# The second attention's keys and values projected during self-attention, and one output product moved ahead of the raw transposes

## The chip, the cores and the metric

The kernel runs on one core of one Trainium2 chip. Times are device microseconds (us) of one execution of the whole kernel; the figure that counts is the median over several executions. Engine names are those of the profile: PE is the matrix engine (PEld its weight loads), DVE the vector engine, ACT the scalar (activation) engine, POOL the GpSimd engine, and SP the engine that issues most of the transfers.

## The reference: what is computed

Two transformer layers over `x` of 16 batches x 128 tokens x 256 features, with a context tensor `ctx_2048` of the same shape:

```
x = x + tanh(g_xattn[0]) * L0_xattn(layernorm(x), ctx_2048)   # 16 heads of 128, self and cross
x = x + tanh(g_ffn[0])   * L0_ffn(layernorm(x))               # gated FFN, 704 wide
x = x + tanh(g_xattn[1]) * L1_xattn(layernorm(x), ctx_2048)   # 32 heads of 8, causal
x = x + tanh(g_ffn[1])   * L1_ffn(layernorm(x))               # top-1 of 8 experts, capacity 256
```

`L0_xattn` attends twice: once to the tokens themselves and once to the context; both results are concatenated, rounded to fp8 and multiplied by `wproj`. `L1_xattn` is the *second attention* of the title. It has 8 key and value groups of 8 features each, 4 query heads to a group. Cut to what matters here:

```
q = (Q @ w_q.T).reshape(B, S, 8, 4, 8)       # Q is the normed x
k = (K @ w_k.T).reshape(B, S, 8, 8)          # K is ctx_2048
v = (V @ w_v.T).reshape(B, S, 8, 8)          # V is ctx_2048
scores = einsum('bnghd,bmgd->bnghm', q, k) / sqrt(8)      # padding and causal mask
out = einsum('bnghm,bmgd->bnghd', softmax(scores), v)
return out @ w_o.T + b_o
```

So the keys and values of the second attention depend on the context and two weights alone, and on nothing that the kernel computes before.

## The kernel before

**Self- and cross-attention (lines 239 to 665).** The work is cut into 32 units: units 0 to 15 are the self-attention of one batch each, units 16 to 31 the cross-attention. A unit takes four steps; the loop at line 626 counts steps `n` from -11 to 135, so that unit u has its scores in the steps n = 4u to 4u+3. Each step handles four heads (`c`, 0 to 3) as a software pipeline: `scores`, `top` (row maximum), `exp`, one step later `recip` and `divide`, two steps later `probs` (transposes of the weights), three later `values`, `smooth` and `quant`, four later `quant_last` (which writes `cat` on POOL), five later `output` (the product with `wproj`, summed over the 16 heads of a unit in one accumulator). Ahead of its scores, a unit is projected in eight blocks of 512 columns, two in a step (`project`, `evict`, `bn`: blocks 0 and 1 are keys, 2 to 5 queries, 6 and 7 values), from step 4u-5 on. When blocks 0 to 5 have their statistics, `rstd` (step 4u-2, a chain of small DVE operations that ends in `q_r`) gives the scale of every head, `mult` (line 454, POOL) applies it to the *raw* blocks, and `heads` (line 463) transposes the raw blocks on PE, keys in step 4u-1, queries in the steps after. These are the "raw transposes".

`output` is called at the end of each step, after `heads`, `heads_q` and the second projection block:

```
            if ab[1]:
                ab[1][0].project(ab[1][1])
                ...
            do(n, 5, "output")
            once(n, 8, "residual")
```

In a step with n % 4 == 3, `output` handles c = 2 of the unit that is one and a half units behind; its operand `cat` is written by the `quant_last` of that same step.

**Order.** The functions are called in the order written out by hand in this loop. The tile framework turns that into one in-order queue for each engine, with semaphores between them; as the trace shows, an engine's order is that of the calls except where the framework let an operation go ahead (in the steps n % 4 == 3, for instance, one projection product stands ahead of the score products although it is called after them). Accumulators live in PSUM pools: two buffers `mm` for projections, two `tr` for transposes, two `sc` for scores, one `pv`, one `acc`.

**First FFN (lines 674 to 732, and 1083 to 1092)**: four groups of four batches, `gate_up` and `down`. In its second group the second attention's first group of four batches is prepared by `front_step`.

**Second attention (lines 904 to 1141).** The loop at line 1107 runs over 64 steps, four to a batch, each with eight heads: `scores`, `top`, `probs` of the step before, `exp`, and in every second step `values`. Every 16 steps a group of four batches is prepared ahead of its use by `front_step`: `load` (context and mask), `norm`, `turn`, and four calls of `qk` (line 949), which project queries (`aq`) and keys (`ak`, in which each key row stands four times, once for each query head of its group). `keys(b)` spreads a batch's keys over the heads with `hmask` (POOL, line 975), projects its values with `av` (line 981), and copies them into one of two padded tiles `vpads` (DVE, line 986). `output` and the `route` generators follow.

**Second FFN (lines 1149 to 1195)**: eight experts, tokens gathered and scattered through HBM.

Of the kernel before, what the change touches and what calls it, by code (L numbers as in the profile page):

```python
# [18 lines left out]
P = 128  # L19
# [16 lines left out]
def flamingo_kernel(  # L36
# [194 lines left out]

    xqx = dram.tile([B, P, KD * P], F32, name="xqx")
    x1 = dram.tile([B, P, DM], F32, name="x1")
    NU = 2 * B


# [2 lines left out]
    with (  # L239
# [346 lines left out]
        units = [Unit(u) for u in range(NU)]  # L586


        loads = {}

        def at(n, f, *args):
# [34 lines left out]
        for n in range(first, last + 1):  # L626
            for m in range(0, B, 4):
                if n == 4 * m - 11:
                    stats(m // 4)
            once(n, -8, "load")  # L630
            for f, args in loads.get(n, ()):
                f(*args)
            ab = [front(n, i) for i in range(2)]
            do(n, 1, "recip")
            do(n, 4, "quant_last")
            do(n, 1, "divide")
            do(n, 0, "scores")
# [233 lines left out]

# [32 lines left out]
    front = {}  # L904

    def load(g):
        cT = gp.tile([P, KD, NT], F32, tag="cT", name="cT")
        nc.gpsimd.dma_start(out=cT, in_=kpn(ctxT)[:, :, g * NT : (g + 1) * NT])
        mi = gp.tile([P, NT], I32, tag="mi", name="mi", bufs=1)
        nc.sync.dma_start(  # L910
            out=mi, in_=mask[g * NT : (g + 1) * NT].partition_broadcast(P)
        )
        comb = gp.tile([P, G, P], BF16, tag="comb", name="comb")
        pad = gp.tile([P, NT], F32, tag="pad", name="pad", bufs=1)
        nc.vector.tensor_scalar(pad, mi, 0.0, NEG, ALU.is_equal, ALU.mult)
# [4 lines left out]
        front[g] = {"cT": cT, "comb": comb}  # L920

    def norm(g):
        rows = [x[b] for b in range(g * G, (g + 1) * G)]
# [22 lines left out]
            nc.scalar.copy(hT[:, k, :], pt.rearrange("p n t -> p (n t)"))  # L946
        front[g]["hT"] = hT

    def qk(g, i, c):

        f = front[g]
        if c == 0:
            f[i] = gp.tile([P, KD, NT], F32, tag="qk"[i], name="qk"[i] + "T")
# [7 lines left out]
        if i == 0:  # L961
            nc.scalar.activation(f[i][:, c, :], pm, AF.Copy, scale=SCALE1)
        else:
            nc.scalar.copy(f[i][:, c, :], pm)

    kbs, vps, es, eTs, oTs, scs, mxs = {}, {}, {}, {}, {}, {}, {}

    def keys(b):
# [4 lines left out]
        kb = ap.tile([P, KD, NQ, P], F32, tag="kb", name="kb")  # L973
        for c in range(KD):
            nc.gpsimd.tensor_tensor(  # L975
                kb[:, c], f[1][:, c, None, tok].to_broadcast([P, NQ, P]),
                hmask[:, :, None].to_broadcast([P, NQ, P]), ALU.mult,
            )
        pm = psum.tile([P, NG, HD], F32, tag="mm", name="ps_mm")
        for k in range(KD):  # L980
            nc.tensor.matmul(
                pm, f["cT"][:, k, tok], av[:, k, :], start=(k == 0), stop=(k == KD - 1)
            )
# [3 lines left out]
        kbs[b], vps[b] = kb, vp  # L987

    def scores(n):

# [10 lines left out]
        with tc.high_priority(offset=100):  # L1001
            for i in range(2):
                rows = slice(32 * (2 * p + i), 32 * (2 * p + i) + 32)
                nc.tensor.matmul(  # L1004
                    s[:, i], f[0][rows, c, tok], kbs[b][rows, c], start=False, stop=True
                )
        scs[n] = s

# [64 lines left out]
    def front_step(g, i):  # L1073
# [193 lines left out]
```

## Time and profile before

| | us |
|---|---|
| median of 3 runs | 1542.24 (1539.53 to 1543.59) |
| the profiled execution | 1540.11 |
| its span in the profile | 1538.2 |
| PE busy | 1388.1 |
| DVE busy | 1052.2 |
| ACT busy | 814.6 |
| POOL busy | 669.5 |

The first score product of self-attention starts at 63.7 us of the span, the first cross product with the context at 473.9, the last output product of cross-attention at 947.6; the first FFN begins at 955.6, the second attention's first scores at 1079.6, its last value products at about 1388; the first gather of the second FFN is issued at 1408.1.

How to read it: the span is what the profiler saw of one execution; the time is measured outside it, in that execution 1.9 us more. Busy time is the union of an engine's instructions, matmul ends are modelled, and the matrix engine's granted clock is given as a share of full speed. The profile's timeline merges neighbouring instructions of one kind (`x4` is four of them) and puts in brackets how long the engine sat idle before them and whose result ended that.

### The profile page before, as it was taken

What the parts mean: (1) busy time and instruction counts of PE and PEld (TensorE: products, weight loads), DVE (VectorE), ACT (ScalarE), POOL (GpSimd) and SP (SyncE); (2) the same over time, 40 slices, a digit from 0 to 9 for tenths busy, and PEclk for the clock granted to TensorE, in tenths of its full rate; (3) what the DMA queues carried; (4) which work ended last, traced back from release to release, by engine and by line L of the source; (5) the groups of instructions that cost most, each with busy time, mean ns of one, the idle gap of its engine ahead of it and who ended that gap; (6) DMA issues with size and microseconds to landing.
All of it is one profiled execution on the core that took longest, in us unless ns stands there. A gap on an engine that the chain in (4) does not pass through costs nothing. (4 is left out here: it accounts for less than half of the span.)

```text
span 1538.2 us, 24640 instructions
## 1 busy us (share of the span) xinstructions
PE 1388.1 (90%) x8612; PEld 1009.7 (66%) x8612; DVE 1052.2 (68%) x2788; ACT 814.6 (53%) x2421; POOL 669.5 (44%) x574
## 2 busy tenths in 40 slices
PE   2778889798897999999999986999999999996998
PEld 1567677677675677777777764555556666664887
DVE  8888878878789777676767765433579797883100
ACT  3656566566556676666666662353355454542121
POOL 4576666666766555556565554120021312111111
PEclk9799999999999999999999998999999999996999
DMA  4300000000013100000000003400210100001662
GB/s 122 112 7 18 28 11 32 15 11 22 11 45 100 44 23 22 11 19 15 18 15 18 8 8 110 141 1 0 83 49 9 50 9 36 9 36 63 194 198 67
DMA packets 51115, 68.67 MB, mean 45 GB/s; under 512 B 5291, under 2 KB 37739, under 8 KB 50992
## 3 DMA queue, kind: packets, MB, share of 16 engines
q1 hardware_dynamic: 36912, 41.31, 9.1%
q10 hardware_dynamic: 11456, 17.63, 3.6%
q0 software_dynamic: 2624, 8.16, 1.5%
q8 instruction: 68, 1.11, 0.3%
q14 instruction: 55, 0.45, 0.1%
HBM read 50.53 MB, written 16.81 MB: 44 GB/s over the span
## 5 line engine op out<-in xcount | busy, mean ns | idle before, releaser
L509 POOL TENSOR_TENSOR e<-e,sums 128x512 f32<-128x512 f32 x128 | 139.7, 1092 | 230.8 <-DVE sums L505 120.8
L497 ACT ACTIVATE e<-ps_sc,mx 128x128 f32<-128x128 f32 x512 | 181.3, 368 | 90.1 <-DVE mx L489 82.7
L454 POOL TENSOR_TENSOR raw<-raw,q_r 128x512 f32<-128x512 f32 x192 | 207.9, 1112 | 34.1 <-DVE q_r L180 33.0
L431 DVE BATCH_NORM_STATS2 q_st<-raw 128x6 f32<-128x128 f32 x768 | 174.1, 279 | 66.9 <-ACT raw L422 66.5
L1020 ACT ACTIVATE e<-ps_sc,mx 128x128 f32<-128x128 f32 x512 | 139.7, 384 | 119.1 <-DVE mx L1011 114.1
L565 PE MATMUL ps_acc<-wp,cat 128*128 128x512 f32 x512 | 160.4, 436 | 17.6 <-POOL cat L227 15.5
L463 PE MATMUL ps_tr<-ident,raw 128*128 128x128 f32 x768 | 121.9, 288 | 46.0 <-POOL raw L454 43.8
L227 POOL TENSOR_TENSOR cat<-e_t,e_e 128x1024 fp32r<-128x1024 bf16 x64 | 136.2, 2128 | 53.7 <-DVE e_t L221 52.1
L481 PE MATMUL ps_sc<-kT,qT 128*128 128x128 f32 x1024 | 140.3, 280 | 15.0 <-ACT qT L472 15.0
L481 PEld LDWEIGHTS ps_sc<-kT,qT 128*128 128x128 f32 x1024 | 131.1, 193 | 33.0 <-ACT qT L472 27.0
L463 PEld LDWEIGHTS ps_tr<-ident,raw 128*128 128x128 f32 x768 | 96.0, 147 | 83.3 <-POOL raw L454 58.2
L519 ACT COPY eT<-ps_tr 128x512 f32<-128x512 f32 x128 | 75.4, 589 | 139.0 <-PE ps_tr L517 138.9
L975 POOL TENSOR_TENSOR kb<-kT,hmask 128x512 f32<-128x512 f32 x32 | 33.6, 1067 | 243.9 <-PE ps_sc L1004 184.6
L565 PEld LDWEIGHTS ps_acc<-wp,cat 128*128 128x128 f32 x512 | 95.9, 194 | 57.4 <-POOL cat L227 22.2
L527 PE MATMUL ps_pv<-eT,vt 128*128 128x256 f32 x512 | 132.1, 379 | 1.0 <-DVE cat_y L538 1.0
L422 ACT COPY raw<-ps_mm 128x512 f32<-128x512 f32 x192 | 113.7, 593 | 27.9 <-PE ps_mm L410 24.8
L527 PEld LDWEIGHTS ps_pv<-eT,vt 128*128 128x128 f32 x512 | 95.9, 189 | 31.2 <-issue 9.0
L538 DVE TENSOR_TENSOR cat_y<-ps_pv,r_sm 128x512 bf16<-128x512 f32 x128 | 87.1, 680 | 39.7 <-PE ps_pv L527 39.5
L472 ACT ACTIVATE qT<-ps_tr,hv 128x512 f32<-128x512 f32 x128 | 100.9, 789 | 21.8 <-PE ps_tr L463 19.8
L497 ACT ACTIVATION_READ_ACCUMULATOR e<-ps_sc,mx 128x1 f32 x512 | 105.3, 206 | 0.0
L489 DVE TENSOR_REDUCE mx<-ps_sc 128x4 f32<-128x512 f32 x128 | 87.2, 681 | 23.6 <-PE ps_sc L481 23.6
L1011 DVE TENSOR_REDUCE mx<-ps_sc 128x8 f32<-128x1024 f32 x64 | 78.2, 1222 | 25.0 <-PE ps_sc L1004 23.4
(228 smaller groups left out, 2807.3 us busy)
## 6 DMA issues: line engine op xcount, KB each, us to landing
w1t<-in_w ACTq DMA_DIRECT2D x8, 1024.0 KB, 5.0
w2t<-in_w ACTq DMA_DIRECT2D x8, 1024.0 KB, 5.6
disp<-empty SPq DMA_DIRECT2D x16, 257.0 KB, 8.5
xe<-disp SPq DMA_DIRECT2D x8, 514.0 KB, 3.6
stage<-in_wprojT SPq DMA_DIRECT2D x16, 256.0 KB, 2.7
xg<-in_x SPq DMA_DIRECT2D x4, 512.0 KB, 3.9
xb<-in_x SPq DMA_DIRECT2D x16, 128.0 KB, 2.1
ctx<-in_ctxT SPq DMA_DIRECT2D x16, 128.0 KB, 2.2
```

The costliest lines, as they stand in the source:

```text
L227: nc.gpsimd.tensor_tensor(dst, t[:, part], e[:, part], ALU.subtract)
L422: nc.scalar.copy(raw.rearrange("p h d -> p (h d)"), pm)
L431: nc.vector.bn_stats(self.st[:, 4 * blk + j, :], self.raws[blk][:, j, :])
L454: nc.gpsimd.tensor_tensor(src, src, self.r[:, 4 * blk : 4 * blk + 4, None].to_broadcast([P, 4, P]), ALU.mult,)
L463: nc.tensor.transpose(pt[:, j, :], src[:, j, :], ident)
L472: nc.scalar.activation(dst, pt, AF.Identity, scale=hv[:, col : col + 1], bias=hv[:, col + 1 : col + 2])
L481: nc.tensor.matmul(pscore[:, j, :], qT[:, j, :], self.kT[:, 2 * c + j // 2, :], start=True, stop=True,)
L497: nc.scalar.activation(e[:, j, :], pscore[:, j, :], AF.Exp, bias=self.mx[:, j : j + 1], accum_out=sums[:, j : j + 1],)
L509: nc.gpsimd.tensor_tensor(e, e, sums[:, :, None].to_broadcast([P, 4, P]), ALU.mult)
L527: nc.tensor.matmul(pv[:, 2 * g : 2 * g + 2, :], self.vt[:, gg * P : (gg + 1) * P], eT[:, 2 * g : 2 * g + 2, :], start=True, stop=True,)
L565: nc.tensor.matmul(self.acc, self.cat[c // 2][:, h % 8, :], wpr[self.cross, c][:, j, :, :], start=(h == 0), stop=(h == 15),)
L1020: nc.scalar.activation(e[:, i, :], s[:, i // NQ, i % NQ, :], AF.Exp, bias=mx[:, i : i + 1])
```

## The change

It has two parts.

1. Keys and values of the second attention are projected inside the loop of self- and cross-attention, one batch at a time, by a new function `kv1(b)`, called in step 4b+3 for the batches 0 to 14 and in step 61 for batch 15, after the first projection block and the statistics, and before `rstd` and the raw transposes. Four steps earlier `load_kv1` loads that batch's context (before batch 0 also the weights; of `akT` only one of the four equal copies of each row). The results are copied out by ACT and stored to two new tensors in HBM, `k1s` and `v1s`. The second attention reads them back: for each group of four batches 16 transfers of eight partitions each repeat the keys for the four heads, and one transfer brings the values. `qk` becomes `queries` and projects queries alone; `keys` loses its products, and its four DVE copies become one POOL copy with a repeated source.
2. In the steps with n % 4 == 3, `output` is called after `rstd` and before `mult` and `heads`; in the other steps it stays where it was.

```diff
+    k1s = dram.tile([NG * HD, B * P], F32, name="k1s")
+    v1s = dram.tile([B * P, NG * HD], F32, name="v1s")
...
+        ak = ap.tile([P, KD, NG * HD], F32, tag="ak", name="ak", bufs=1)
+        av = ap.tile([P, KD, NG * HD], F32, tag="av", name="av", bufs=1)
+        cxs = {}
+        kv1_at = {4 * b + 3: b for b in range(B - 1)}
+        kv1_at[4 * (B - 1) + 1] = B - 1
+
+        def load_kv1(b):
+            if b == 0:
+                for k in range(KD):
+                    nc.sync.dma_start(
+                        out=ak[:, k].rearrange("p (g d) -> p g d", d=HD),
+                        in_=akT[k * P : (k + 1) * P, :].rearrange(
+                            "p (g h d) -> p g h d", h=NH // NG, d=HD
+                        )[:, :, 0, :],
+                    )
+                nc.sync.dma_start(out=av, in_=kpn(avT))
+            cxs[b] = ap.tile([P, KD, P], F32, tag="ctx", name="ctx")
+            nc.sync.dma_start(out=cxs[b], in_=kpn(ctxT)[:, :, b * P : (b + 1) * P])
+
+        def kv1(b):
+            cx = cxs.pop(b)
+            tok = slice(b * P, (b + 1) * P)
+            pm = ps_mm([P, P + NG * HD])
+            for k in range(KD):
+                nc.tensor.matmul(
+                    pm[: NG * HD, :P], ak[:, k, :], cx[:, k, :], start=(k == 0), stop=(k == KD - 1)
+                )
+            for k in range(KD):
+                nc.tensor.matmul(
+                    pm[:, P:], cx[:, k, :], av[:, k, :], start=(k == 0), stop=(k == KD - 1)
+                )
+            ko = ap.tile([NG * HD, P], F32, tag="ko", name="ko")
+            vo = ap.tile([P, NG * HD], F32, tag="vo", name="vo")
+            nc.scalar.copy(ko, pm[: NG * HD, :P])
+            nc.scalar.copy(vo, pm[:, P:])
+            nc.sync.dma_start(out=k1s[:, tok], in_=ko)
+            nc.sync.dma_start(out=v1s[tok, :], in_=vo)
...
             if ab[0]:
                 ab[0][0].bn(ab[0][1])
+            if n + 4 in kv1_at:
+                load_kv1(kv1_at[n + 4])
+            if n in kv1_at:
+                kv1(kv1_at[n])
             once(n, -2, "rstd")
+            if n % 4 == 3:
+                do(n, 5, "output")
             for blk in range(2):
                 once(n, -2, "mult", blk)
                 once(n, -1, "heads", blk)
...
-            do(n, 5, "output")
+            if n % 4 != 3:
+                do(n, 5, "output")
...
-    ak = cq.tile([P, KD, DM], F32, name="ak")
-    av = cq.tile([P, KD, NG * HD], F32, name="av")
...
-    nc.sync.dma_start(out=ak, in_=kpn(akT))
-    nc.sync.dma_start(out=av, in_=kpn(avT))
...
     def load(g):
-        cT = gp.tile([P, KD, NT], F32, tag="cT", name="cT")
-        nc.gpsimd.dma_start(out=cT, in_=kpn(ctxT)[:, :, g * NT : (g + 1) * NT])
+        tok = slice(g * NT, (g + 1) * NT)
+        kT = gp.tile([P, KD, NT], F32, tag="k", name="kT")
+        for r in range(0, P, HD):
+            q = r // 32
+            nc.sync.dma_start(
+                out=kT[r : r + HD],
+                in_=k1s.rearrange("(c q d) t -> q d c t", q=4, d=HD)[q][:, :, tok],
+            )
+        v = gp.tile([P, G, NG * HD], F32, tag="v", name="v")
+        nc.sync.dma_start(out=v, in_=v1s[tok, :].rearrange("(b t) n -> t b n", t=P))
...
-    def qk(g, i, c):
+    def queries(g, c):
...
-        w, src = ((aq, f["hT"]), (ak, f["cT"]))[i]
...
-                pm, w[:, k, c * P : (c + 1) * P], src[:, k, :],
+                pm, aq[:, k, c * P : (c + 1) * P], f["hT"][:, k, :],
...
-        pm = psum.tile([P, NG, HD], F32, tag="mm", name="ps_mm")
-        for k in range(KD):
-            nc.tensor.matmul(
-                pm, f["cT"][:, k, tok], av[:, k, :], start=(k == 0), stop=(k == KD - 1)
-            )
-        vp = vpads[b % 2]
-        for i in range(NQ):
-            nc.vector.tensor_copy(vp[:, :, i, HD * i : HD * i + HD], pm)
+        vp = vpads[b % 2][:]
+        nc.gpsimd.tensor_copy(
+            bass.AP(vp.tensor, vp.offset, [vp.ap[0], [P, NG], [32 + HD, NQ], [1, HD]]),
+            f["v"][:, j, :].rearrange("p (g d) -> p g d", d=HD)[:, :, None, :].to_broadcast(
+                [P, NG, NQ, HD]
+            ),
+        )
...
-        elif 5 <= i < 9:
-            qk(g, (i - 5) // 2, (i - 5) % 2)
+        elif 5 <= i < 7:
+            queries(g, i - 5)
```

More of the change, by code (lines that the diff above doesn't have):

```diff
@@ L919, in load @@
         )
-        front[g] = {"cT": cT, "comb": comb}
+        front[g] = {"k": kT, "v": v, "comb": comb}
     def norm(g):
@@ L947, in turn @@
         front[g]["hT"] = hT
-    def qk(g, i, c):
+    def queries(g, c):
         f = front[g]
         if c == 0:
-            f[i] = gp.tile([P, KD, NT], F32, tag="qk"[i], name="qk"[i] + "T")
-        w, src = ((aq, f["hT"]), (ak, f["cT"]))[i]
+            f["q"] = gp.tile([P, KD, NT], F32, tag="q", name="qT")
         pm = psum.tile([P, NT], F32, tag="mm", name="ps_mm")
@@ L957, in qk @@
             nc.tensor.matmul(
-                pm, w[:, k, c * P : (c + 1) * P], src[:, k, :],
+                pm, aq[:, k, c * P : (c + 1) * P], f["hT"][:, k, :],
                 start=(k == 0), stop=(k == KD - 1),
             )
[L961 to L964, printed above, removed]
+        nc.scalar.activation(f["q"][:, c, :], pm, AF.Copy, scale=SCALE1)
     kbs, vps, es, eTs, oTs, scs, mxs = {}, {}, {}, {}, {}, {}, {}
@@ L975, in keys @@
             nc.gpsimd.tensor_tensor(
-                kb[:, c], f[1][:, c, None, tok].to_broadcast([P, NQ, P]),
+                kb[:, c], f["k"][:, c, None, tok].to_broadcast([P, NQ, P]),
                 hmask[:, :, None].to_broadcast([P, NQ, P]), ALU.mult,
             )
-        pm = psum.tile([P, NG, HD], F32, tag="mm", name="ps_mm")
-        for k in range(KD):
-            nc.tensor.matmul(
-                pm, f["cT"][:, k, tok], av[:, k, :], start=(k == 0), stop=(k == KD - 1)
-            )
-        vp = vpads[b % 2]
-        for i in range(NQ):
-            nc.vector.tensor_copy(vp[:, :, i, HD * i : HD * i + HD], pm)
-        kbs[b], vps[b] = kb, vp
+        vp = vpads[b % 2][:]
[5 more added lines that the diff above has]
+        )
+        kbs[b], vps[b] = kb, vpads[b % 2]
     def scores(n):
@@ L1004, in scores @@
                 nc.tensor.matmul(
-                    s[:, i], f[0][rows, c, tok], kbs[b][rows, c], start=False, stop=True
+                    s[:, i], f["q"][rows, c, tok], kbs[b][rows, c], start=False, stop=True
                 )
```

## The prediction

> **What bounds the kernel now.** I read the windows view first, to see which engine limits which stage, then the timelines of PE and POOL over one unit of each stage.
>
> ```profile
> core 0: us, PE busy (x) PEld busy (x) DVE busy (x) ACT busy (x) POOL busy (x), PEclk, DMA share, GB/s
> 200.00:300.00 100.00, 88.81 (x512) 74.46 (x510) 83.61 (x241) 61.57 (x194) 65.57 (x52) 0.98 0.06 21
> 600.00:700.00 100.00, 98.93 (x511) 73.02 (x510) 74.74 (x220) 64.32 (x198) 58.25 (x46) 1.00 0.06 17
> 1200.00:1300.00 100.00, 99.86 (x1046) 60.60 (x1045) 79.66 (x178) 51.58 (x180) 23.12 (x22) 1.00 0.10 35
> ```
>
> Self-attention (first row) leaves PE idle 11 us in 100; cross-attention and the second attention leave none. So PE work taken from the third row may pay and PE work put into the first may be free, if it lands in the holes. Where they are, PE's timeline over self-attention's step n = 43 shows:
>
> ```profile
> 358.77 1.02 PE L527 MATMUL ps_pv<-eT,vt 128*128 128x256 f32 x4
> 362.27 0.66 PE L463 MATMUL ps_tr<-ident,raw 128*128 128x128 f32 x4 [2.48 <-POOL raw L454]
> ...
> 364.69 0.60 PE L463 MATMUL ps_tr<-ident,raw 128*128 128x128 f32 x4
> 365.05 1.17 PE L565 MATMUL ps_acc<-wp,cat 128*128 128x512 f32 x4
> ```
>
> One hole of 2.48 us in each unit: the key transposes wait for POOL's raw. The output product stands behind them, at 365.05. POOL's timeline says what else was ready:
>
> ```profile
> 358.51 2.12 POOL L227 TENSOR_TENSOR cat<-e_t,e_e 128x1024 fp32r<-128x1024 bf16 x1
> 361.18 5.03 POOL L454 TENSOR_TENSOR raw<-raw,q_r 128x512 f32<-128x512 f32 x5 [0.55 <-DVE q_r L180]
> ```
>
> `cat`, the output product's operand, is done at 360.63, before the first raw starts. The hole also costs clock; windows of 7 us from the key transposes of two units:
>
> ```profile
> 307.01:314.01 7.00, 7.00 (x36) 5.97 (x37) 2.64 (x11) 4.79 (x12) 5.93 (x6) 0.76 0.00 0
> 335.19:342.19 7.00, 6.66 (x41) 5.63 (x42) 2.55 (x9) 5.23 (x16) 5.93 (x6) 1.00 0.00 0
> ```
>
> Of 14 units (n = 3 to 55) eight show 0.76 to 0.79 there, the others 1.00.
>
> **Output product moved.** A unit repeats in 27.08 us (335.19 to 362.27). Its chain: from the key transposes PE runs without a hole to the last query block, whose statistics lead through DVE to `q_r`, POOL's raw, and the next key transposes. Four products leave the running part, worth 1.01 us (337.97 to 338.98 in PE's timeline of the unit before), and go into the hole. With c = 2 the step issues nothing else (the `xb` transfer belongs to c = 0), so it is moved past PE's queue alone. DVE idles 4.6 us in that part, so it can follow. At n = 7 to 55, thirteen units: -13.1 us. At n = 59 the trace has an output product ahead of the transposes already, and later units are cross-attention: 0.
>
> **kv1 in the loop.** Eight matmul records a batch. The key half is 128 columns wide like the scores, of which eight take 0.89 us to the next instruction: 0.45; the value half has L981's shape, four in 0.40 (1156.72 to 1157.12). With the output product 1.86 us of the 2.48 are filled, so 0 in the 15 batches up to n = 59 (at n = 3 the holes are 0.87 and 0.34, at n = 59 PE waits 2.71 for `cat`); if the hole were gone, 0.85 x 15 = 13 us. Batch 15 (step 61) has no such hole: +1. Two ACT copies, by the 128x128 activate row at most 0.37 each, by the 128x512 copy row 0.59: I take 0.37, since the shape is nearer. They stand before the exponentials, where ACT idles 2.06 us in such a step (until 276.10): 0, else 0.7 x 16 = 11. Their PSUM buffer is one of two `mm`; the next block that needs it comes a step later. On SP, three issues of 0.32 us a batch; the stores wait for ACT, and behind them stand only `xb` and `x1` transfers that nothing waits for within a step: 0. The weights (`akT` in pieces of 32 bytes) are issued once, four steps ahead: 0. The last context loads share two buffers with cross-attention's and come a step or two later; that stage change already has holes: 0, at worst 3.
>
> **Clock.** Twelve units from 108.18 to 446.76 take 338.58 us; at 27.08 they would take 325.0. About 1 us in three of them is statistics of `x` (137.52 to 165.57 is 28.05 without a drop). The other 10.6 us belong to seven drops, 1.5 us each; eight cost 12. Bounds: 0, and 8 x 7 x 0.24 = 13.4. The Trainium skill ("TensorE: Matmul & The Clock Gate", Why this matters for your kernels) says that the clock falls if PE idles over about 3 us between bursts. By that rule 2.48 us would be harmless and this term 0; the windows show that it is not. I take 12, because only about 0.6 us of the hole is left. Self-attention in all: -13.1 - 12 + 1 = -24 us.
>
> **First FFN.** The first group's key projection, 1020.47 to 1023.91 with PE always busy, goes: -3.4.
>
> **Second attention.** Key projections of three groups: each 1.82 us (1142.69 to 1144.51) and 1.78 (1147.93 to 1149.71). Not all of it comes back, nor the values' 16 x 0.40, for PE's timeline shows what happens where no filler stands:
>
> ```profile
> 1323.94 0.56 PE L981 MATMUL ps_mm<-av,cT 128*128 128x64 f32 x4
> ...
> 1325.92 1.09 PE L1031 MATMUL ps_tr<-ident,e 128*128 128x128 f32 x8
> ...
> 1332.31 0.59 PE L997 MATMUL ps_sc<-comb,identb 128*128 128x512 bf16 x2
> ...
> 1333.89 1.73 PE L1031 MATMUL ps_tr<-ident,e 128*128 128x128 f32 x8
> ```
>
> With value products before the scores the transposes take 1.09 us, without them 1.73: 0.64 us of waiting for `e`. A step without filler takes PE 2.51 us (1329.80 to 1332.31), and DVE as much (`mx` 1.23, `eT` 1.28). So the values give about nothing (0 to -6.4); I take -1, since four DVE copies go too (9.8 us in all, beside a DVE at 80%). The second key product of a group has the same neighbours: 1.78 - 0.5 = 1.3. Keys: 3 x (1.82 + 1.3) = -9.4. Sum -10.4.
>
> **Cover.** POOL's new copy (128x256) costs 1.25 us by L934, the nearest row; 16 make 20 us on a POOL at 23%, each wanted five steps later: 0. It waits for the value products that read its buffer, as DVE did; behind it stand key spreads wanted two steps later. Key loads: 16 SP issues of 0.32 us a group, 5.1, ten steps (some 50 us) ahead. The skill ("DMA: Bandwidth & Descriptors", Rules for kernel authors) speaks against them: transfers under 64 KB are mostly overhead, and an outermost dimension of eight confines one to eight engines; these are 32 KB and eight partitions. At the 6.3 us that the 64 KB `av` load takes to land, one after another, a group would need 101 us, 50 more than it has, and three groups 150. But the trace has transfers overlap: SP issues sixteen `disp` writes of 257 KB in 16.34 us, and each takes 8.5 to land. So I take 0; no row here shows a load of eight partitions.
>
> **Sum.** -24 - 3.4 - 10.4 = -38 us against the profiled execution's 1540.1 (span 1538.2 + 1.9): 1502. The median of the runs is 2.1 higher, so 1504. About 0.3% is what measurement can tell from no change.
>
> **Rivals.** *A, as summed (0.60)*: 1504, own range 1492 to 1516.
> *B, the wait moves (0.17)*: raw hangs on `q_r`, a chain on a DVE that is 84% busy. If it slips by what PE gains, the move gives nothing and the clock half of its drops: -14 - 5, so 1523. For it: `q_r` ends 8.7 us after the last statistics (352.41 to 361.10). Against: DVE's 4.6 us of idling.
> *C, not done as said (0.07)*: the framework may let other work ahead (L410 x1 stands before the scores it is called after), leave the hole, and put kv1 on the running part: +13 - 14, 1541.
> *D, slower (0.16)*: in cross-attention POOL does the raw first. PE's and POOL's timelines there:
>
> ```profile
> 669.65 1.03 PE L527 MATMUL ps_pv<-eT,vt 128*128 128x256 f32 x4
> 670.51 1.04 PE L463 MATMUL ps_tr<-ident,raw 128*128 128x128 f32 x8
> 671.38 1.02 PE L410 MATMUL ps_mm<-wxk,ctx 128*128 128x512 f32 x2
> ```
>
> ```profile
> 666.26 4.81 POOL L454 TENSOR_TENSOR raw<-raw,q_r 128x512 f32<-128x512 f32 x4 [1.27 <-DVE q_r L180]
> 671.04 2.12 POOL L227 TENSOR_TENSOR cat<-e_t,e_e 128x1024 fp32r<-128x1024 bf16 x1
> ```
>
> If the product really stands before the transposes there, PE waits from 670.51 for a `cat` done at 673.16: 2.65 us x 16 = 42, and clock drops in 8 of 14, 16 x 0.57 x 1.5 = 14: +56 - 38, 1560. It decides from 38 / 16 = 2.4 us a unit. Against it: L410 x2 stands before the query transposes called earlier, so the framework lets ready work pass, and it held the fourth raw, hence `cat` behind it, for not ready then.
>
> **Numbers.** Faster is A and B, same C, slower D. The range reaches from the bounds (values -6, more of the idle filled: 1485) over A, B and C to 1546.
>
> **What would show it.** Self units of about 26 us, L565 ahead of L463 in steps n % 4 == 3, a raw wait under 1 us there, clock 1.00 in all those windows; the L957 products from `cT` and L981 gone, the L1031 groups after short steps still stretched. Wrong: L565 waiting for `cat` in cross-attention, units still 27 to 29 us, or scores waiting for `kb` or `k1s`.

## Result and profile after

| | before | after |
|---|---|---|
| median of 6 runs each, us | 1541.13 (1536.95 to 1543.59) | 1578.19 (1575.31 to 1584.64) |
| profiled execution, its span | 1540.11, 1538.2 | 1575.31, 1573.6 |

The changed kernel is slower: ratio 1.0247, 95% interval 1.0224 to 1.0270. The forecast was 1504 with a range to 1546. Four landmarks of the two traces say where the 35.4 us of span went (a stage's length is the distance between its first and last transfer, or score product; the landmarks are read to 0.1 us):

| stage | before | after | difference |
|---|---|---|---|
| self-attention (first to last store of `xqx`) | 411.5 | 421.2 | +9.7 |
| cross-attention (first to last load of `xx`) | 410.7 | 450.9 | +40.2 |
| from there to the first FFN's first product | 111.2 | 120.4 | +9.2 |
| first FFN, to the first score of second attention | 124.6 | 120.2 | -4.4 |
| second attention, first to last score product | 298.8 | 279.6 | -19.2 |

(The rest is the overlap of the first two stages, +0.3, and the tail, -0.4, and rounding.) The third row is the last cross units, still at work when the last load is issued. So second attention gave more than was forecast, self-attention lost 10 us instead of winning 24, and cross-attention lost nearly 50.

The windows view after, for the same three stretches as before (columns: window, its length, busy time of PE, PEld, DVE, ACT and POOL with the instructions in brackets, granted clock, DMA share, GB/s):

```profile
200.00:300.00 100.00, 87.95 (x494) 70.74 (x495) 84.64 (x224) 56.98 (x182) 61.68 (x51) 0.98 0.08 25
600.00:700.00 100.00, 91.44 (x448) 67.08 (x446) 64.10 (x191) 58.44 (x182) 53.22 (x42) 0.97 0.05 14
1200.00:1300.00 100.00, 99.70 (x1162) 61.18 (x1163) 85.77 (x162) 54.78 (x199) 24.29 (x26) 1.00 0.08 27
```

Cross-attention (second row) had no idle PE before and the full clock; now 8.6 us in 100 are idle, and the granted clock is 0.97. Self-attention is as full as before although PE got more to do. Where the hole stood, PE's timeline of the self unit of step n = 39 now shows:

```profile
341.38 1.03 PE L530 MATMUL ps_pv<-eT,vt 128*128 128x256 f32 x4
342.34 0.65 PE L617 MATMUL ps_mm<-ctx,ak 128*64 128x128 f32 x4
342.92 0.66 PE L621 MATMUL ps_mm<-av,ctx 128*128 128x64 f32 x4
343.39 1.18 PE L568 MATMUL ps_acc<-wp,cat 128*128 128x512 f32 x4
344.84 0.66 PE L466 MATMUL ps_tr<-ident,raw 128*128 128x128 f32 x4 [0.27 <-POOL raw L457]
```

The projections (L617, L621), 1.05 us to the start of the next product, and the moved product (L568) fill the hole, 0.27 us are left: the edit is made as meant. The clock drops of self-attention are gone too, here for the units that answer to the two shown before:

```profile
316.21:323.21 7.00, 6.36 (x38) 4.92 (x39) 2.72 (x12) 5.63 (x17) 5.93 (x6) 1.00 0.12 30
344.84:351.84 7.00, 6.66 (x41) 5.38 (x42) 3.11 (x12) 5.63 (x19) 5.93 (x6) 1.00 0.10 26
```

All fourteen windows of this kind have 1.00; before it was six of fourteen. Yet self-attention is not shorter: the unit from 335.19 to 362.27, which had no drop before, took 27.08 us, and now (344.84 to 372.98) it takes 28.14. PE's waits between 63.5 and 420 us (columns: who waited for what, us in total, times, longest), before:

```profile
PE ps_tr L463 <- POOL raw L454: 36.6, 23, 3.8
PE ps_sc L481 <- ACT qT L472: 11.4, 13, 1.7
PE ps_acc L565 <- POOL cat L227: 2.7, 1, 2.7
```

and after:

```profile
PE ps_sc L484 <- ACT qT L475: 27.3, 23, 3.5
PE ps_tr L466 <- POOL raw L457: 7.4, 21, 0.6
```

The wait for `raw` went (-29 us), a wait of the score products for `qT` took its place (+16). In cross-attention the timelines of PE and POOL show the rest:

```profile
668.57 1.03 PE L530 MATMUL ps_pv<-eT,vt 128*128 128x256 f32 x4
671.79 1.20 PE L568 MATMUL ps_acc<-wp,cat 128*128 128x512 f32 x4 [2.20 <-POOL cat L227]
```

```profile
664.85 4.81 POOL L457 TENSOR_TENSOR raw<-raw,q_r 128x512 f32<-128x512 f32 x4 [1.27 <-DVE q_r L180]
669.62 2.12 POOL L227 TENSOR_TENSOR cat<-e_t,e_e 128x1024 fp32r<-128x1024 bf16 x1
```

There POOL does four raw blocks before `cat`; the moved product stands in front of transposes that could run, and PE waits 2.20 us or more for `cat` in fourteen units. The granted clock falls there too, after some of these waits and not after others; two windows of 7 us from the moved product on:

```profile
641.64:648.64 7.00, 6.99 (x29) 4.80 (x30) 0.58 (x4) 2.92 (x4) 2.94 (x3) 0.76 0.00 0
671.79:678.79 7.00, 6.99 (x38) 5.20 (x39) 1.62 (x6) 3.93 (x8) 2.94 (x3) 1.00 0.00 0
```

Of the fourteen windows of this kind in the trace nine have 0.76; before, cross-attention had 1.00 throughout (473.9 to 844.4 us). From one load of `xx` to the next it is 26.5 us before, 28.5 after without a drop and 30.2 with one. That is the prediction's rival D, with both of its terms.

### The profile page after: what moved, and what is told of

Same layout as the page of the kernel before. It is cut to its first block, busy times and chain, and to the rows that moved or that the text cites. A ratio compares the mean times of both kernels' runs of the same rounds, so it can differ in the third digit from the quotient of the medians.

```text
span 1573.6 us, 24879 instructions
## 1 busy us (share of the span) xinstructions
PE 1405.3 (89%) x8644; PEld 1014.0 (64%) x8644; DVE 1065.7 (68%) x2724; ACT 808.8 (51%) x2445; POOL 675.1 (43%) x586
## 5 line engine op out<-in xcount | busy, mean ns | idle before, releaser
L568 PE MATMUL ps_acc<-wp,cat 128*128 128x512 f32 x512 | 156.2, 429 | 46.5 <-POOL cat L227 46.3
L484 PE MATMUL ps_sc<-kT,qT 128*128 128x128 f32 x1024 | 143.5, 284 | 33.6 <-ACT qT L475 33.4
L568 PEld LDWEIGHTS ps_acc<-wp,cat 128*128 128x128 f32 x512 | 96.2, 194 | 82.9 <-POOL cat L227 55.1
L466 PE MATMUL ps_tr<-ident,raw 128*128 128x128 f32 x768 | 124.6, 292 | 18.8 <-POOL raw L457 14.6
L466 PEld LDWEIGHTS ps_tr<-ident,raw 128*128 128x128 f32 x768 | 99.7, 151 | 60.4 <-POOL raw L457 34.4
L1080 PEld LDWEIGHTS ps_tr<-ident,e 128*128 128x128 f32 x512 | 57.6, 140 | 57.9 <-ACT e L1069 21.8
```

What stands on the lines that cost most here:

```text
L466: nc.tensor.transpose(pt[:, j, :], src[:, j, :], ident)
L484: nc.tensor.matmul(pscore[:, j, :], qT[:, j, :], self.kT[:, 2 * c + j // 2, :], start=True, stop=True,)
L568: nc.tensor.matmul(self.acc, self.cat[c // 2][:, h % 8, :], wpr[self.cross, c][:, j, :, :], start=(h == 0), stop=(h == 15),)
```

## Experiments

All times are medians; a ratio is against the kernel before on the same chip, with its 95% interval.

### Which edit, in which stage

The two parts were made apart, and the move in self-attention apart from cross-attention.

```diff
 # e1: the projections, no product moved
-            if n % 4 == 3:
-                do(n, 5, "output")
...
-            if n % 4 != 3:
-                do(n, 5, "output")
+            do(n, 5, "output")
 # e2: the kernel before, product moved in all units: condition n % 4 == 3
 # e3: the changed kernel, e4: the kernel before, both with the condition
+            if n % 4 == 3 and n < 60:
```

> The changed kernel with all output products back in their old place; keys and values projected during self-attention stay. Theory M (the move did all the harm: in cross-attention PE stands at the moved product for cat, and in self-attention the shifted product reorders ACT so that qT stands behind exps that wait for mx): 1541 minus the 15 us that the rest of the span lost, so about 1526, self units as before (27.4 us) or at most 0.3 us longer, cross units as before (25.7 us). Theory K (the ten microseconds in self-attention belong to the projections, 1.05 us of PE and two ACT copies in each unit): cross as before, self still 10 us or more longer, about 1536 to 1542.

> The kernel before with only the output product moved ahead of the raw transposes, in self and cross alike; second attention untouched. Theory M: plus 40 in cross and plus 10 in self, about 1591. Theory K: plus 40 in cross, and in self the 13 us that the prediction gave to the move come in, about 1568.

> The changed kernel with the product moved in self-attention alone (steps below 60). Theory M and theory K both: the 40 us of cross-attention are gone, 1578 minus 40 gives about 1538, self still 28.1 us per unit. The rival that cross-attention's loss does not come from the moved product (a leftover of the shifted schedule): stays near 1578.

> The kernel before with the product moved in self-attention alone, no projections. Theory M: plus 10, about 1551, with PE waits for ACT qT near 30 us in self-attention. Theory K: minus 13, about 1528, with PE waits for qT as before (12 us).

| run | us | ratio | self | cross |
|---|---|---|---|---|
| projections only | 1533.04 | 0.9947 (0.9930 to 0.9963) | 423.0 | 414.4 |
| move only, everywhere | 1592.21 | 1.0332 (1.0314 to 1.0349) | 412.3 | 449.6 |
| projections, move in self | 1535.00 | 0.9956 (0.9939 to 0.9973) | 425.2 | 414.8 |
| move in self only | 1545.28 | 1.0027 (1.0016 to 1.0038) | 411.2 | 411.5 |

The move in cross-attention costs 43 us with the projections (1578 - 1535) and 47 without (1592 - 1545). In self-attention neither theory held: the move alone is worth nothing there (411.2 against 411.5), not -13 and not +10; the projections alone cost 11.5 us. About 4 us more go in the change from self to cross: between the second and third load of `xx` there are 56.3 us before and 60.3 with the projections, and the later intervals agree within about 0.1.

### Cross-attention: is it POOL's order?

```diff
             def mult_q(self, c):
+                if self.cross and c == 0:
+                    return
+                if self.cross and c == 1:
+                    self.first = done["cat"]
+                    self.mult(2)
                 self.mult(c + 2)
 # and in mult, for the blocks 2 to 5 of a cross unit:
+                    behind(ins, self.first)      # POOL keeps this order
```

> The changed kernel with one order changed on POOL in cross-attention: cat goes behind the two key raws and ahead of the four query raws (the query raws are told to follow it). Theory D (PE stands at the moved product because cat comes behind four raws of 1.20 us): the wait for cat falls from 2.2 us a unit to about 0.3, cross units get 1.5 to 2 us shorter, 1578 minus 25 to 35, so 1543 to 1553. Rival (the product stands in the way there whatever cat does, for example by its own 1.1 us or by a later q chain): at most 10 us back, 1568 or more.

Measured: 1538.86, ratio 0.9984 (0.9977 to 0.9991), 39 us less than the changed kernel. POOL's timeline of a cross unit in this run:

```profile
657.27 2.37 POOL L471 TENSOR_TENSOR raw<-raw,q_r 128x512 f32<-128x512 f32 x2 [1.27 <-DVE q_r L187]
660.27 2.12 POOL L234 TENSOR_TENSOR cat<-e_t,e_e 128x1024 fp32r<-128x1024 bf16 x1 [0.63 <-DVE e_t L228]
```

and PE's:

```profile
662.44 1.20 PE L584 MATMUL ps_acc<-wp,cat 128*128 128x512 f32 x4 [0.42 <-POOL cat L234]
```

With the product still in its new place, but `cat` behind two raws instead of four, the wait is 0.42 us in place of 2.20. So the loss in cross-attention is POOL's order, and not the product's place by itself. (The gain is above the expected 25 to 35 us: these counted the waits alone, and the nine clock drops went with them, 1.7 us each; the granted clock from 488 to 864.6 us is 1.00 again.)

### Self-attention: where the filled hole's time went

To see it, a self unit is cut along the chain that ends in `q_r`. Means over thirteen units, from the starts and ends in each trace's timeline: A, from the key transposes to the start of ACT's copy of the last query block; B, from there to the start of `q_dif`; C, to the end of `q_var`; D, from the start of ACT's last step of the rsqrt to the end of `q_r` on DVE. Two constant pieces (0.82 and 1.18 us) complete the unit.

| kernel | A | B | C | D | unit |
|---|---|---|---|---|---|
| before | 15.89 | 3.28 | 2.73 | 4.37 | 28.25 |
| move in self only | 15.16 | 3.75 | 2.88 | 4.41 | 28.19 |
| projections only | 16.31 | 3.88 | 2.62 | 4.33 | 29.13 |
| after | 16.04 | 3.75 | 2.92 | 4.28 | 29.00 |
| before, short divide | 15.93 | 3.02 | 2.63 | 3.81 | 27.37 |
| move, short divide | 14.84 | 3.09 | 2.78 | 3.84 | 26.55 |
| projections, short divide | 15.74 | 3.25 | 2.57 | 3.77 | 27.32 |

These means hold units with and without a clock drop (a drop lengthens A by some 1 to 1.6 us). One unit, the one that ends at the key transposes of step n = 43, has no drop in any of the seven kernels:

| kernel | A | B | C | D | unit |
|---|---|---|---|---|---|
| before | 15.34 | 3.06 | 2.50 | 4.18 | 27.08 |
| move in self only | 15.26 | 3.64 | 3.06 | 4.12 | 28.08 |
| projections only | 15.35 | 3.79 | 2.50 | 4.19 | 27.82 |
| after | 15.32 | 3.64 | 3.05 | 4.12 | 28.14 |
| before, short divide | 15.34 | 2.90 | 2.52 | 3.56 | 26.31 |
| move, short divide | 14.62 | 3.13 | 3.06 | 3.50 | 26.30 |
| projections, short divide | 15.33 | 3.11 | 2.50 | 3.56 | 26.49 |

On average the move shortens A by 0.73 us, and B and C give 0.62 of it back. But most of the 0.73 is clock drops that went. In the unit without one A gets only 0.08 us shorter, B and C get 1.14 us longer, and the unit 1.0 us. (Six of the thirteen units have no drop before: the move makes five of them 1.0 us longer and leaves one as it was; the seven with a drop get 0.8 us shorter on average.) B and C are DVE's. The groups view names the operations; between 63.5 and 420 us, before:

```profile
L220 DVE TENSOR_SCALAR e_e<-e_e 128x1024 bf16<-128x1024 bf16 x37 | 16.5, 445 | 0.2
L440 DVE SCALAR_TENSOR_TENSOR q_var<-q_st 128x24 f32<-128x24 f32 x13 | 4.5, 350 | 0.0
```

and with the move in self-attention:

```profile
L220 DVE TENSOR_SCALAR e_e<-e_e 128x1024 bf16<-128x1024 bf16 x37 | 30.0, 812 | 0.6
L440 DVE SCALAR_TENSOR_TENSOR q_var<-q_st 128x24 f32<-128x24 f32 x13 | 8.7, 667 | 0.0
```

The same instructions take nearly twice as long (the number after the busy time is the mean in ns). The timeline says beside what:

```profile
322.68 1.36 POOL L509 TENSOR_TENSOR e<-e,sums 128x512 f32<-128x512 f32 x1 [0.72 <-DVE sums L505]
323.18 1.15 DVE L220 TENSOR_SCALAR e_e<-e_e 128x1024 bf16<-128x1024 bf16 x1
```

POOL's divide starts 0.5 us before `e_e`, and `e_e` takes 1.15 us; in the kernel before, `e_e` starts 0.22 us ahead of the divide (351.19 and 351.41) and takes 0.43. The long `q_var`, in C, stands beside another POOL operation, `xx`:

```profile
355.48 0.68 POOL L227 TENSOR_TENSOR xx<-e_t,e_e 128x256 fp32r<-128x256 bf16 x1
355.51 0.70 DVE L440 SCALAR_TENSOR_TENSOR q_var<-q_st 128x24 f32<-128x24 f32 x1
```

In every unit of both traces `q_var` takes 0.7 us where it stands beside `xx` and 0.2 where it does not. In three runs the divide was made short (one head in four is divided, the other three are left undivided), with the queues' order as it was; in a fourth only the order around it was changed.

```diff
 # short divide (e7: before, e8: move in self only, e9: projections only)
+                k = 4 if self.cross else 1
                 nc.gpsimd.tensor_tensor(
-                    e, e, sums[:, :, None].to_broadcast([P, 4, P]), ALU.mult
+                    e[:, :k], e[:, :k], sums[:, :k, None].to_broadcast([P, k, P]), ALU.mult
                 )
 # e11: projections, move in self; recip keeps behind e_e of cat_y on DVE
-                nc.vector.reciprocal(sums, sums)
+                ins = nc.vector.reciprocal(sums, sums)
+                if not self.cross and "cat" in seen:
+                    behind(ins, seen["cat"])
```

> The kernel before; POOL's divide in self-attention is done for one head in four only (the other three stay undivided), so it takes some 0.3 us in place of 1.04 to 1.36; the order of all queues is as before. It is the base of the next run. In the kernel before the divide mostly stands clear of e_e (0.43 us), so a gain of 0 to 8 us is expected, 1533 to 1541.

> The kernel before with the product moved in self-attention alone, with the same short divide. Theory C (the 13 us that the move takes out of PE's running part are given back on DVE, where e_e takes 1.15 us instead of 0.40 and q_var 0.71 instead of 0.20 because POOL's divide now runs beside them): the move shows its gain here, 10 to 15 us below the run with the short divide alone, about 1520 to 1528. Rival O (they are given back by the order on ACT, qT behind four exponentials): this run is within 5 us of the run with the short divide alone.

> The changed kernel with all output products in their old place (the projections alone), and POOL's divide in self-attention done for one head in four only, the other three left undivided; order of all queues as in the run with the projections alone. To be read against the kernel before with the same short divide (1527). Theory C (the projections fit the hole; the 11.5 us that self-attention lost with them come from POOL's divide falling on e_e, 1.15 in place of 0.43 us): with the rest of the span 20 us shorter it gives about 1507 to 1511. Theory K (they cost 0.7 us a unit by their own PE and ACT work): 1527 + 11.5 - 20, about 1518 to 1520.

> The kernel with the projections and the product moved in self-attention alone, all arithmetic kept, with one order changed on DVE: in self-attention the reciprocal that releases POOL's divide follows e_e of the quantization of cat_y instead of standing before it. Theory C: e_e back at about 0.43 us in two of three places, the part from the last raw to q_dif back from 3.65 to about 3.0 us or the next part shorter, 0.5 to 0.8 us in each of 16 units: 1535 minus 8 to 13, 1522 to 1527. Rival (POOL's divide, late by 1 us, becomes what PE waits for, or DVE only loses elsewhere): 1533 to 1540.

| run | us | ratio | self |
|---|---|---|---|
| before, short divide | 1526.87 | 0.9904 (0.9888 to 0.9921) | 399.9 |
| move in self, short divide | 1517.86 | 0.9843 (0.9826 to 0.9859) | 388.8 |
| projections, short divide | 1506.07 | 0.9763 (0.9743 to 0.9783) | 398.6 |
| projections, move in self, recip behind `e_e` | 1534.75 | 0.9962 (0.9948 to 0.9976) | 421.6 |

With a short divide the move wins 11.1 us in self-attention (399.9 to 388.8) where it won 0.3, and the projections cost -1.3 us where they cost 11.5. So what the two edits cost hangs on the divide's length: in the unit without a drop the move costs 1.0 us with the long divide and nothing with the short one, the projections 0.74 and 0.18. That it acts through `e_e` is argued from the lines above; a short divide also empties POOL's queue earlier. The move's own 1.01 us do not come in even then: A is 0.72 us shorter, but C is 0.54 longer, with `q_var` still beside `xx`, and B 0.23. Most of the 11.1 us is the clock, for seven of the thirteen units have a drop in the kernel before with the short divide, and two with the move.

The divide itself was worth more than expected: nearly 15 us in the kernel before, half a microsecond a unit of it in D, where L178 waits beside POOL's `cat`, and `cat` starts after the divide. That forecast was a miss, and the last run is another: `e_e` is back at 0.40 to 0.43 us in all 36 cases (63.5 to 420 us) and the ordinary units are 0.6 us shorter, but the whole is not faster (1534.75 against 1535.00). Lengthened `e_e` is a part of the loss; that it is all of it was wrong: `q_var` still takes 0.70 us beside `xx`, and the long units of the next paragraph stay long.

Two units do not belong to this: after the change, those with the statistics of four batches take 31.15 and 32.63 us. In one of them:

```profile
289.95 0.21 ACT L175 ACTIVATE x_a<-v 128x4 f32<-128x4 f32 x1 [3.60 <-DVE v L310]
290.07 0.76 ACT L475 ACTIVATE qT<-ps_tr,hv 128x512 f32<-128x512 f32 x1
290.88 1.87 PE L484 MATMUL ps_sc<-kT,qT 128*128 128x128 f32 x8 [3.51 <-ACT qT L475]
```

ACT waits 3.60 us for `v` with `qT` queued behind, PE waits 3.51 us for `qT`, and the next products run at a lower clock (1.87 us in place of 1.16). `v` is late: four of DVE's small operations ahead of it take 0.96 us each while POOL does its raws. Two runs moved that rsqrt in ACT's queue.

```diff
 # e6: the statistics' second rsqrt behind the next step's exponentials
+        if after is not None:
+            behind(ins, after)           # after: last exp of step 4m - 8
 # e13: behind qT and one raw copy instead, and recip behind e_e as above
```

> The kernel with projections and the product moved in self-attention alone, and one more order: on ACT the second rsqrt of the statistics of x is told to follow the exponentials of the next step, so that it no longer stands ahead of qT while it waits 3.6 us for DVE. Theory S (two or three self units pay 4 us each for that place in ACT's queue): 1535 minus 8 to 13, so 1522 to 1527, the long units of 33.5 us down to about 29. Rival (those units are long because of the statistics' DVE work itself): no change, 1533 to 1537.

> The same with the statistics' second rsqrt placed on ACT behind qT and one raw copy, ahead of the next exponentials (one step earlier than in the run where it followed them and PE then waited 2.6 us for xh). If both terms add up: the gain of the run with the reciprocal behind e_e and another 4 to 8 us, 1515 to 1522, a candidate for the best version. If the statistics' delay is DVE's own (five small operations of 0.96 us beside POOL's raw): no more than the reciprocal's order alone gives.

Measured: 1530.95, ratio 0.9936 (0.9919 to 0.9953), and 1528.55, ratio 0.9908 (0.9889 to 0.9928). In the first the wait for `qT` is gone, but PE waits 2.6 us for `xh` in three later places instead, and the long units stay near 32 us: half a miss. The second has no unit above 30 us and is 6.5 us under the run without these orders, less than the two terms promised.

### What sets a self unit

If the chain through `q_r` sets the unit, a shorter chain must shorten it without any work taken from PE. The refining step of `q_r` (L177 to L180, part D) was left out in self-attention.

```diff
         nc.scalar.activation(r, a, AF.Exp, scale=-0.5)
+        if not newton:
+            return r
...
+                self.r = rsqrt(small, var, 24, "q", 2, newton=bool(self.cross))
```

> The kernel before, but in self-attention q_r is taken from ACT's result alone; its refining step, four DVE operations on 128x24 (4.2 us from ACT's result to q_r, 2.05 of them L178 beside POOL's cat), is left out. Theory Q (a self unit repeats in the time of the chain last raw, q_st, q_dif, q_var, q_r, POOL's raw, key transposes, and the hole on PE is what is left over): 2.5 to 3.4 us off each of 16 units and the clock drops gone, 1541 minus 40 to 60, 1481 to 1501. Rival P (PE's own work sets the unit and the hole is only its order): at most 10 us, 1531 or more.

> The same with the product moved in self-attention. Theory Q: with the chain short, PE has no hole ahead of the key transposes, so where the product stands does not matter, or it waits there for cat as in cross-attention: 0 to 30 us above the run without the move. Rival P: 10 us below it, as with the short divide.

> The version with both orders mended (projections, product moved in self-attention, 1528) with the refining step left out as well. Theory Q: PE is then what bounds self-attention, and the projections' 1.05 us a unit cost 17 us there while the rest of the span gains 20 us; about 3 us below or up to 30 us above the kernel before without the refining step (the moved product may wait for cat).

> The projections with every output product in its old place, and the refining step of q_r left out in self-attention. Theory Q, as amended by the last runs (the chain through q_r sets the unit until cat comes too late for the output product at its old place): the kernel before without the refining step took 1518; the rest of the span gains 20 us; the projections' 1.05 us stand ahead of the key transposes, where no hole is left, and cost 0 to 17 us, less what cat's wait (12 us there) absorbs: 1500 to 1515, faster than both kernels of the case. If the moved products and not the projections made the run with both orders and no refining step slow (1542), it lands there; if the projections did, near 1540.

| run, without the refining step | us | ratio | self |
|---|---|---|---|
| before | 1517.98 | 0.9859 (0.9842 to 0.9875) | 386.0 |
| move in self only | 1547.68 | 1.0054 (1.0037 to 1.0071) | 415.2 |
| projections, move in self, both orders | 1541.73 | 1.0011 (1.0002 to 1.0020) | 427.6 |
| projections, product in its old place | 1507.57 | 0.9791 (0.9775 to 0.9808) | 398.8 |

Four small DVE operations are worth 25.5 us of self-attention; the ordinary unit falls from 27.08 to 25.73 us. It is less than the 40 to 60 expected, because the next thing is late at once: POOL now does three raws ahead of `cat`, and PE's waits for `cat` rise from 2.7 to 12.2 us at the product's old place. Nor is all of the 25.5 us the chain's: 1.35 us a unit make some 18 us in thirteen units, and clock drops that went are in the rest (granted clock 0.99 over the stage, 0.96 before). And with the chain short, the moved product does in self-attention what it does in cross-attention: it waits for `cat`, and the granted clock is 0.96 again. PE's timeline of the second run:

```profile
281.40 2.08 PE L567 MATMUL ps_acc<-wp,cat 128*128 128x512 f32 x4 [3.75 <-POOL cat L229]
```

The last run, the projections without any move, is 33 us under the kernel before (1507.57 and 1540.68), so it was the moved product that made the third run slow. It is under both kernels of the case, but it leaves the refining step out; like for like it is 10 us under the first run (1517.98). In self-attention the projections cost 13 us here too (386.0 to 398.8).

### Second attention: keys or values

```diff
 # e15: projections only, but values computed in second attention as before
+        pm = psum.tile([P, NG, HD], F32, tag="mm", name="ps_mm")
+        for k in range(KD):
+            nc.tensor.matmul(
+                pm, f["cT"][:, k, tok], av2[:, k, :], start=(k == 0), stop=(k == KD - 1)
+            )
 # and four DVE copies into vpads; e16: one ACT copy and POOL's spread instead
```

> The kernel with the projections alone (1533), but second attention computes its values again as the kernel before does (four products of 128x64 and four DVE copies a batch, its context loaded anew); its keys still come from memory. It splits the second attention's gain, which was 17 us where the prediction had 10.4 (keys 9.4, values 1). If the values are worth what the prediction said: within 2 us of 1533. If the part that the prediction missed is the values': 1539 to 1542.

> As the run with the values kept in second attention (1541), but the spread into vpad is done by POOL from one ACT copy of the products, so that the four DVE copies a batch are gone and only the 64 small products of the values stay on PE. It splits that run's 8 us. If they were PE's products (16 batches of 0.40 to 0.56 us are 6.4 to 9.0): stays at 1539 to 1542. If they were the DVE copies (16 batches of 0.61 us are 9.8, behind which mx and eT stand): comes back to 1533 to 1535.

Measured: 1540.72 (0.9989, 0.9981 to 0.9998) and 1541.00 (1.0007, 1.0000 to 1.0014), against 1533.04 with the values from memory. From first to last score product it is 281.4 us without them, 287.8 and 289.7 with them. So the values' products are worth 6 to 8 us, on PE: with DVE's copies gone (and one short ACT copy a batch in their place) and the products kept, nothing came back. The keys are the rest, 298.8 - 287.8 = 11.0. These are single traces; with both from memory the length varies between 279 and 283 us from run to run, so the split is good to some 2 us.

## Why the prediction was wrong

**Rival D came true, in both terms.** It had 2.65 us x 16 = 42 us for waits in cross-attention and 14 us for clock drops. Fourteen units wait 2.20 to 2.65 us, 32 us in all; the nine drops, at 1.7 us, make 15. That is 47 us, and by the runs the move costs 43 to 47 there: the waits were overpriced, the drops were not. (D's sum was 1560 and 1578 was measured, mainly because D kept the -24 us of self-attention.) The two POOL lines that showed it were on the page. The step that failed is the argument against it: that the framework lets ready work pass, and so would place the transposes first. In the changed kernel it did not; PE kept the order of the calls. Why the framework held the product for ready in time, no trace shows.

**The moved product, -13.1.** The four products left the running part and filled the hole, as said. What failed is the sentence that DVE idles 4.6 us in that part and can follow. DVE's idle time was no slack: where the shifted `e_e` met POOL's divide and `q_var` met `xx`, they took 0.5 to 0.7 us longer, so `mx`, the exponentials and `qT` came later, and PE waited for `qT`. A unit without a clock drop got 1.0 us longer and not 1.01 shorter. This was rival B's mechanism, the wait moving to the chain, which had 0.17. With the short divide the 1.0 us is gone, but the gain does not come in.

**The projections in the loop, 0.** Right for the hole, wrong for the unit: self-attention got 11.5 us longer with the divide as it is, and 1.3 us shorter with a short one, where four clock drops fewer hide 0.18 us a unit. Looked at was where the work lands on PE and ACT, and not what a shift of half a microsecond does to two engines that collide. On PE they take 1.05 us a batch and not 0.85. In the five units without a drop in either kernel B grows by 0.7 to 1.0 us and A by at most 0.03; the mean of A (+0.42) comes from the other units. Next to the moved product, ordinary units differ from those with the move alone by 0.05 to 0.9 us, and the two statistics units by 3.2 and 4.7. For batch 15 and the stage change the text had +1 and "at worst 3"; it was 4.

**Clock, -12.** The drops went, in eight of eight windows, so the trace was rightly followed against the Trainium skill's rule of about 3 us of idling ("TensorE: Matmul & The Clock Gate", Why this matters for your kernels). The time came too: with the move alone the seven units that had a drop are 0.8 us shorter although the move costs 1.0, so the drops are worth some 7 x 1.8 = 13 us (an estimate from these two figures). But the move's term, with its sign reversed, took as much: 411.2 us against 411.5. That the two nearly cancel is chance. And the sum put nothing down for the drops that the move brings to cross-attention; only D did.

**First FFN, -3.4: measured -4.4. Second attention, -10.4: measured -19.2.** The keys' 9.4 measured 11.0. The term that was mis-sized is the values: taken as -1, because transposes stretch where no filler stands (1.73 us in place of 1.09), they are worth 6 to 8. In the changed kernel most of the stretched transposes take 1.48 to 1.52 us, so the stretch gives back less than was taken from the trace of before.

**Cover, 0.** Right. POOL's spread took 0.45 us on average, a third of the 1.25 that the nearest row gave; the key loads cost SP 0.30 us each, and no score product waited for `kb`, `k1s` or `v1s`. The Trainium skill's rows on transfers under 64 KB and on a short outermost dimension ("DMA: Bandwidth & Descriptors", Rules for kernel authors) bear on how long such loads take; no trace here shows when they land, only that no product waited.

**What stays open.** Why `q_var` came to stand beside `xx`, and why the run with `recip` behind `e_e` gains 3.6 us in self-attention (421.6 against 425.2) and nothing in its median. Its second attention, where nothing was changed, is 1.8 us longer in the trace, so differences of a few us between single traces are not resolved here.

## What to carry to other kernels

A product that is moved ahead of other work on an in-order engine must have its operand ready there in every stage that runs the same loop: read the producer's queue in each of them, and take a wait seen there times the number of units, with the clock drops that follow it. Here the hole on PE was what a chain on other engines left over: 2 us of work put into it brought nothing by itself, because the chain moved along, while leaving four small operations out of the chain brought 1.35 us a unit. So follow the chain before filling the hole. Where DVE and POOL work side by side, count on a shift of half a microsecond to change how long their operations take. And compare units without a clock drop with each other: a mean over both kinds mixed a loss of 1.0 us with a gain from the clock here, and showed neither.

## What the hardware showed that was not expected

- DVE operations slow down beside POOL operations: `e_e` (128x1024 bf16) 0.40 to 0.43 us ahead of POOL's divide and 1.15 beside it; `q_var` (128x24) 0.20, and 0.71 beside `xx`; the statistics' 128x4 operations 0.15 and 0.96; L178 (128x24) 2.05 beside `cat`, which itself takes 2.12.
- The granted clock fell after shorter idling than the holes of before. In the run with the projections alone, three of the eight windows that followed a hole of 1.31 or 1.32 us had a clock of 0.76; in the kernel before with the short divide, two of eight after 1.85 or 1.86 us; in the projections with the short divide, none of eight after 0.67 to 0.69 us, but one of two after 0.85. The hole's length alone does not decide: in the kernel before, 2.48 or 2.49 us gave a drop in three of eight. In the changed kernel's cross-attention, waits of 2.20 to 2.65 us came with nine drops, where the stage had none before.
- The copy with a repeated source on POOL (128x256) took 0.40 us in most of its 16 executions (mean 0.45, longest 0.93); a scale and shift of the same size takes 1.23 to 1.25 on average.
